# Scheduling weights chosen per stretch of 40 planned microseconds in a two-layer transformer kernel

## The chip, the cores and the metric

The kernel runs on one core of a Trainium2 chip. The core has a matrix engine (TensorE, here PE; its weight loads are listed as PEld), VectorE (DVE), ScalarE (ACT), GpSimd (POOL) and SyncE (SP), which issues most DMAs. Each engine works through its own queue in the order in which the program lists its instructions, and waits on semaphores for the others. The metric is the device time of one execution in microseconds (us), as the median of several runs. A profile comes from one further execution; its span runs from the first to the last recorded instruction.

## What is computed

Two layers over x of shape (1, 2048, 256), in float32. Each has an attention of 16 heads of width 16 with a causal mask, and a gated feed-forward part with int8 weights; each of the four parts sits between two layer norms and is added to x:

```python
x = x + _layernorm(_L0_attn_ref(_layernorm(x, axis=-1), L0_attn_W_d_q, ...), axis=-1)
x = x + _layernorm(_L0_ffn_ref(_layernorm(x, axis=-1), ...), axis=-1)
x = x + _layernorm(_L1_attn_ref(_layernorm(x, axis=-1), ...), axis=-1)
x = x + _layernorm(_L1_ffn_ref(_layernorm(x, axis=-1), ...), axis=-1)
return x
...
scores = jnp.einsum('bhqd,bhkd->bhqk', q, k) / math.sqrt(Hd)
causal = jnp.triu(jnp.full((S, S), -jnp.inf, dtype=scores.dtype), k=1)
scores = scores + causal[None, None]
attn = jax.nn.softmax(scores, axis=-1)
out = jnp.einsum('bhqk,bhkd->bhqd', attn, v)
...
gate = jax.nn.silu(_qmatmul(x, w_gate, s_gate))
up = _qmatmul(x, w_up, s_up)
fuse = gate * up
return _qmatmul(fuse, w_down, s_down)
```

Layer 0's attention draws q and k from low-rank projections with norms and a rotation of their own; layer 1's is the plain one.

## The kernel before

**Tiling.** The 2048 rows are four chunks `c` of 512. Heads are worked on in four groups `g` of four, so that an attention has 16 units `(c, g)`, in the order of `UNITS`: two of chunk 0, all of chunks 1, 2 and 3, then the other two of chunk 0. For each unit, two passes are made:

- *Maxima* (`maxima`, `block`). Blocks of q times k (L766, after two mask products at L762 on the diagonal) go to one PSUM bank each, and VectorE reduces each bank to row maxima (L774). A block uses one half (a "lane") of the array's rows, lane 0 or lane 1; blocks of the two lanes can run at the same time. Unit `(c, g)` has 16c full blocks and ten small ones. POOL splits the maxima into three bf16 parts (L804 to L808), PE turns them (L820) and ACT copies them out (`mrow`, L824).
- *Weighting* (`weighted`). For each of its 4(c+1) key tiles, two score ops subtract the maxima and form the scores (L852 and L857, in two banks), ACT takes the exponential (L863, into `pt`, a ring of six), POOL masks the diagonal ones (L867), and one "weigh" multiplies by the values (L874, eight matmuls). At the end of a unit the result is copied (L882), turned (L887) and divided (L894 to L896).

PE ops have a mode: "row" (maxima and scores), "col" (weighs), "full" (all else). Around these, a chunk's projection (norm, flips at L548, products at L632, `stacked` at L572 and L574) writes q and k to DRAM in SP's stores at L584, and SP loads them back in another layout (`load_stack`, L595) into K and one of three Q buffers. The feed-forward part multiplies at L1027 (gate and up) and L993 (down), with ACT, VectorE and POOL between them (L1034 to L1039). The end of one stage overlaps the start of the next: layer 1's first projection and first maxima are planned inside layer 0's feed-forward part.

**The planner.** All this work is given as ops to a `Plan`, one for each of the four stages (attention 0, feed-forward 0, attention 1, feed-forward 1). An op has an engine, a booked duration in us, a rank (when it is wanted; one unit of attention is 1.0), and buffers it reads, writes or holds. `order` walks through planned time: at each step it works out when each ready op could start (`at`), from its inputs' planned ends, the buffers and PSUM banks that come free, and its engine; for PE with a booked cost for a change of mode (`SWITCH`). It takes the engine of the op that can start first, and among that engine's ops that can start at most `near` us later it picks the one of the least `rank + waiting * (at - first)`. That order of ops is then the order of the instructions on every engine's queue, SP's and POOL's among them. Nothing of it is computed on the chip.

Booked durations that are spoken of below: a score op nq/1110 (0.461 for 512 columns), a weigh nq/590 (0.868), a full maxima block 0.233, its reduction 0.61, the exponential 0.1 + nq/620; a store of q or k 0.6 per part and 3.0 to land, a load of a stack 1.8 and 2.5 to land; `SWITCH` 0.23 into row, 0.1 into col, 0.2 into full.

`run` plans each stage 15 times, with five values of `near` and three of `waiting`, and keeps the pair of the shortest planned stage.

Of the kernel before, what the change touches and what calls it, by code (L numbers as in the profile page):

```python
# [81 lines left out]
class Ring:  # L82
# [3 lines left out]
        self.slots, self.at, self.ordered = [None] * n, 0, ordered  # L86
        self.asked, self.given = [], 0

    def soonest(self, b, others, later):

        if self.ordered and self.asked[self.given + others] is not b:
            return None
        old = self.slots[(self.at + others) % len(self.slots)]
        users = [u.end for u in old.users] if old else [-1.0]
        return None if None in users else max(users)
# [7 lines left out]
class Banks:  # L103
# [15 lines left out]
        at = [self.ready(i) for i in range(len(self.slots))]  # L119
        return [(max(at[i:i + k]), i) for i in range(len(at) - k + 1) if None not in at[i:i + k]]  # L120

    def pairs(self):

        return sum(self.ready(i) is None and self.slots[i].banks == 2 for i in range(len(self.slots))) // 2

    def soonest(self, b, others, later):


        if b.banks == 2 and (self.asked[self.given] is not b or self.pairs() == self.limit):
            return None  # L130
        if later and b.banks == 1:
            used = sum(self.ready(i) is None and self.slots[i].banks == 1 for i in range(len(self.slots)))
            if used + others >= self.singles:
                return None
        free = sorted(t for t, _ in self.choices(b.banks))
        return free[others] if len(free) > others else None

    def give(self, b, now):
# [8 lines left out]
class Places:  # L147
# [9 lines left out]
        users = [b.users if b else () for b in self.slots]  # L157
        return [(max((u.end for u in us), default=-1.0), i) for i, us in enumerate(users) if all(u.end is not None for u in us)]

    def soonest(self, b, others, later):  # L160

        free = sorted(t for t, _ in self.choices())
        others += self.left if later else 0
        return free[others] if len(free) > others else None

# [13 lines left out]
class Plan:  # L179
# [7 lines left out]
    free, mode = {}, None  # L187
    LAG = {"DVE": 0.08, "ACT": 0.1, "PE": 0.2}

    NEAR, WAITING = (0.05, 0.08, 0.11, 0.14, 0.17), (0.05, 0.1, 0.2)  # L190

    def __init__(self):
        self.ops = []
# [16 lines left out]
        self.ops.append(o)  # L210
        return o

    def order(self, near, waiting, emit=False):

        rings = {b.ring for o in self.ops for b in o.bufs if b.ring is not None}
        before = [(r, list(r.slots), r.at, r.given) for r in rings]
        free, mode, left, follow, ready = dict(Plan.free), Plan.mode, {}, {}, []
        for o in self.ops:
            o.end = None
            for b in o.bufs:  # L220
                b.given = b.tile is not None
        for o in self.ops:
            left[o] = sum(d.end is None for d in o.after)
            for d in o.after:
                follow.setdefault(d, []).append(o)
            if left[o] == 0:
                ready.append(o)
        done = 0
        while ready:
            best = []  # L230
            lowest = {2: min((o.rank for o in ready if o.pair and not o.pair.given), default=math.inf),
                      3: min((o.rank for o in ready if o.wide and not o.wide.given), default=math.inf)}
            for o in ready:
                at = max((d.end + self.HOP for d in o.after), default=0.0)
                wanted = {}
                for b in o.bufs:
                    if b.ring is None or b.given:
                        continue
                    others = wanted.get(b.ring, 0)
                    wanted[b.ring] = others + 1  # L240
                    soonest = b.ring.soonest(b, others, o.rank > lowest[3 if b.banks == 3 else 2])
                    if soonest is None:
                        break
                    at = max(at, soonest + self.HOP)
                else:
                    if o.engine == "PE":
                        lanes, more = (o.lanes, 0.0) if o.mode == mode else ((0, 1), self.SWITCH[o.mode] + o.load - self.LOAD)
                        at = max([at + o.load] + [free.get(("PE", x), 0.0) + more for x in lanes])
                    else:
                        at = max(at, free.get(o.engine, 0.0))  # L250
                    best.append((at, o))
            assert best, "nothing can start"
            first = min(best, key=lambda p: p[0])
            at, o = min((p for p in best if p[1].engine == first[1].engine and p[0] <= first[0] + near),
                        key=lambda p: (p[1].rank + waiting * (p[0] - first[0]), p[0]))
            for b in o.bufs:
                if b.ring is not None and not b.given:
                    b.ring.give(b, at)
                b.given = True
                if emit:  # L260
                    b.t
            if emit:
                o.fn()
            if o.engine == "PE":
                mode = o.mode
                for x in (0, 1):
                    free["PE", x] = at + o.us if x in o.lanes else max(at, free.get(("PE", x), 0.0))
            else:
                free[o.engine] = at + o.us
            o.end = at + o.us + o.lag  # L270
            done += 1
            ready.remove(o)
            for n in follow.get(o, ()):
                left[n] -= 1
                if left[n] == 0:
                    ready.append(n)
        assert done == len(self.ops)
        if emit:
            Plan.free, Plan.mode = free, mode
        else:  # L280
            for r, *state in before:
                r.slots, r.at, r.given = state
        return max(o.end for o in self.ops)

    def run(self):

        tried = [(self.order(near, waiting), near, waiting) for near in self.NEAR for waiting in self.WAITING]
        self.span = self.order(*min(tried)[1:], emit=True)


@with_exitstack
def kernel(ctx: ExitStack, tc: tile.TileContext, x_in, cols_in, rows_in, wd_in, wuq_in, rot_in,
# [646 lines left out]
    class FeedForward:  # L939
# [283 lines left out]
```

## Time and profile before

| | |
|---|---|
| median of 3 runs | 1301.8 us (1301.77 to 1302.59) |
| the profiled execution's own time | 1301.22 us |
| its span | 1299.5 us |
| mean granted clock of TensorE | 0.973 |
| first and last weigh (L874) of attention 0 | 85.1 and 540.5 us |
| first and last weigh of attention 1 | 711.2 and 1179.5 us |

The weighs mark the stages: attention 0 runs to about 560 us, feed-forward 0 to about 700, attention 1 to about 1195, feed-forward 1 to the end, with overlaps.

How to read the views: the page lists, for each engine, its busy time and its number of instructions; the slices show 40 equal parts of the span, each digit a busy share in tenths. A row by window gives the window, its length, then the busy time and count of PE, PEld, DVE, ACT and POOL, then the granted clock, the DMA share and GB/s. A row of waits names who waited for whom, the total in us, how often, and the longest. The timeline and the chain give start, length, engine, line and count. Matmuls are pipelined, so that the time from one's start to the next's start is shorter than the recorded length.

### The profile page before, as it was taken

How to read it: one execution, taken by the hardware profiler on the slowest of the kernel's cores; microseconds unless marked ns; L12 is line 12 of the kernel's file. 1: busy time of each engine (PE TensorE's matmuls, PEld its weight loads, DVE VectorE, ACT ScalarE, POOL GpSimd, SP SyncE). 2: the span in 40 equal slices, each digit the busy share in tenths (PEclk: the TensorE clock that was granted, in tenths of full speed). 3: DMA queues.
4: the chain of work that ended last, by engine and by line, in shares of the span. 5: the costliest groups of instructions: out<-in, count | busy, mean ns of one | idle time of the engine just before them, and what ended most of it. 6: DMA issues, size and time to landing. Idle time of an engine off the chain costs nothing.

```text
span 1299.5 us, 22976 instructions
## 1 busy us (share of the span) xinstructions
PE 1213.0 (93%) x8888; PEld 683.8 (53%) x8888; DVE 902.0 (69%) x1714; ACT 792.0 (61%) x1100; POOL 333.6 (26%) x640
## 2 busy tenths in 40 slices
PE   4889999999999999989977999999999999998995
PEld 3655554544444444568755555454445444445884
DVE  4579888888987972264445878978898888334442
ACT  3344665576676678776433656556655777885653
POOL 6021211211102102375423211121101201134564
PEclk8889999999999999999997999999999999998998
DMA  5554260000000000000164051022000000000000
GB/s 153 178 179 128 68 195 17 18 17 17 2 16 18 17 1 18 26 25 1 39 215 120 1 163 33 17 90 74 18 17 18 17 1 18 17 1 1 1 33 33
DMA packets 43486, 65.70 MB, mean 51 GB/s; under 512 B 10739, under 2 KB 15440, under 8 KB 43376
## 3 DMA queue, kind: packets, MB, share of 16 engines
q1 hardware_dynamic: 43040, 63.80, 15.8%
q8 instruction: 70, 1.15, 0.4%
q10 hardware_dynamic: 288, 0.31, 0.1%
q0 software_dynamic: 48, 0.11, 0.1%
q14 instruction: 40, 0.33, 0.1%
HBM read 41.14 MB, written 23.07 MB: 49 GB/s over the span
## 4 chain that ended last, share of the span: by engine, by line
PE 70%; DVE 15%; ACT 5%; issue 3%; DMA 3%; POOL 2%; SPq 2%; POOLq 0%; ACTq 0%; DVEq 0%
PE banks L874 17%; DVE pm L774 12%; PE banks L852 10%; PE banks L766 10%; PE banks L857 8%; PE banks L632 8%; PE banks L1027 7%; PE banks L993 3%; ACT pt L863 3%; PE banks L762 3%; PE banks L548 1%; DMA sc_q<-wide 1%; PE banks L887 1%; ACT wide L523 1%; DMA x<-in_x_dram 1%
## 5 line engine op out<-in xcount | busy, mean ns | idle before, releaser
L774 DVE TENSOR_REDUCE pm<-banks 128x1 f32<-128x512 f32 (+1 forms) x1088 | 672.9, 681 | 154.9 <-PE banks L766 145.9
L863 ACT ACTIVATE pt<-banks 128x1024 f32<-128x1024 f32 (+3 forms) x640 | 544.3, 900 | 267.1 <-PE banks L857 240.3
L857 PE MATMUL banks<-Q,K 64*128 64x512 f32 (+3 forms) x1248 | 322.2, 519 | 0.0
L766 PE MATMUL banks<-K,Q 64*128 64x128 f32 (+2 forms) x1728 | 308.5, 358 | 10.8 <-DMA Q<-sc_q 7.1
L874 PE MATMUL banks<-pt,V 128*32 128x512 f32 (+3 forms) x2560 | 301.7, 544 | 0.5 <-DVE pm L774 0.2
L852 PE MATMUL banks<-mrow,sel 64*128 64x512 bf16 (+3 forms) x1280 | 248.3, 354 | 13.0 <-ACT pt L863 8.4
L766 PEld LDWEIGHTS banks<-K,Q 64*128 64x128 f32 x1728 | 200.2, 189 | 89.3 <-DVE pm L774 44.0
L852 PEld LDWEIGHTS <-sel 64*128 64x128 bf16 x1280 | 77.8, 93 | 258.6 <-issue 246.2
L867 POOL TENSOR_SCALAR_AFFINE_SELECT pt<-pt 128x256 f32<-128x256 f32 x256 | 102.8, 406 | 324.9 <-ACT pt L863 322.8
L857 PEld LDWEIGHTS banks<-Q,K 64*128 64x128 f32 x1248 | 136.2, 195 | 3.6 <-issue 2.8
L1027 PE MATMUL banks<-F,F 128*128 128x512 f32 x512 | 130.7, 400 | 1.8 <-DVE fu L1036 1.8
L1027 PEld LDWEIGHTS banks<-F,F 128*128 128x128 f32 x512 | 96.9, 191 | 22.5 <-DVE fu L1036 2.2
L804 POOL TENSOR_SCALAR mx<-best 128x16 bf16<-128x16 f32 x32 | 9.4, 295 | 362.5 <-DVE best L799 362.4
L1036 DVE SCALAR_TENSOR_TENSOR fu<-banks,cols,sl 128x512 f32<-128x512 f32 x64 | 47.4, 749 | 73.1 <-ACT sl L1034 40.4
L874 PEld LDWEIGHTS banks<-pt,V 128*32 128x32 f32 x2560 | 51.4, 108 | 84.4 <-issue 62.7
L1039 POOL TENSOR_TENSOR fl<-fu,fh 128x512 fp32r<-128x512 f32 x64 | 81.9, 1291 | 47.6 <-ACT fh L1038 47.6
L762 PE MATMUL banks<-mask,half 64*128 64x512 bf16 x256 | 68.8, 397 | 0.3
L1038 ACT CAST fh<-fu 128x512 fp32r<-128x512 f32 x64 | 39.5, 621 | 32.5 <-DVE fu L1036 30.8
L993 PE MATMUL banks<-fl,F 128*128 128x512 f32 x128 | 52.3, 408 | 4.8 <-POOL fl L1039 4.8
L993 PE MATMUL banks<-fh,F 128*128 128x512 f32 x128 | 53.2, 416 | 2.3 <-DVE fu L1036 2.3
L1034 ACT ACTIVATE sl<-banks,cols 128x512 f32<-128x512 f32 x64 | 43.2, 688 | 12.2 <-PE banks L1027 12.0
L824 ACT COPY mrow<-banks 128x512 bf16<-128x512 bf16 x32 | 18.7, 591 | 47.9 <-PE banks L820 47.9
(122 smaller groups left out, 954.5 us busy)
## 6 DMA issues: line engine op xcount, KB each, us to landing
K<-sc_k SPq DMA_DIRECT2D x128, 128.0 KB
Q<-sc_q SPq DMA_DIRECT2D x120, 128.0 KB
sc_q<-wide SPq DMA_DIRECT2D x48, 256.0 KB
sc_k<-wide SPq DMA_DIRECT2D x32, 256.0 KB
x<-in_x_dram SPq DMA_DIRECT2D x4, 512.0 KB
out_dram<-x SPq DMA_DIRECT2D x4, 512.0 KB
f<-in_ffn_dram SPq DMA_DIRECT2D x2, 768.0 KB
F<-sc_q SPq DMA_DIRECT2D x8, 128.0 KB
```

What stands on the lines that cost most here:

```text
L632: nc.tensor.matmul(s.t[:, at:at + n], a, b, start=start, stop=stop)
L762: nc.tensor.matmul(s.t.rearrange("p (d k) -> p d k", k=P), half16[b, x, :], mask_qk[b, x, :, :], start=x == 0, stop=False)
L766: nc.tensor.matmul(s.t[:, to:to + k], qb.t[b, i, t * P:(t + 1) * P], layer.K(kc)[b, 2 * g + i, k0:k0 + k], start=not masked, stop=not mask ...
L774: nc.vector.tensor_reduce(dst, src, AX.X, ALU.max)
L852: nc.tensor.matmul(s.t[:, e, 0:nq], sel[b:b + 64, i, :], mrow.t[b:b + 64, off:CH], start=True, stop=False)
L857: nc.tensor.matmul(s.t[:, e, 0:nq], layer.K(kt // TPC)[b:b + 64, 2 * g + i, k * P:(k + 1) * P], qb.t[b:b + 64, i, off:CH], start=False, st ...
L863: plan.op("ACT", 0.1 + nq / 620, lambda s=s, pt=pt, nq=nq: nc.scalar.activation(pt.t[:, :, 0:nq], s.t[:, :, 0:nq], AF.Exp, scale=scale), r ...
L867: plan.op("POOL", 0.41, lambda pt=pt: nc.gpsimd.affine_select(out=pt.t[:, :, 0:P], in_=pt.t[:, :, 0:P], compare_op=ALU.is_ge, fill=0.0, ba ...
L874: nc.tensor.matmul(av.t[32 * j:32 * j + 32, off:CH], Vs[kt // TPC][:, kt % TPC, DV * h:DV * h + 32], pts[kt, j // 2].t[:, j % 2, 0:nq], st ...
L993: nc.tensor.matmul(dn[dh].t, wdn[:, fc, dh * P:(dh + 1) * P], halves[fc][j].t, start=fc == 0 and j == 0, stop=fc == 7 and j == 1)
L1027: nc.tensor.matmul(s.t[:, i, :], w[:, cc, fc * P:(fc + 1) * P], xT[j].t[:, cc, :], start=n == 0, stop=n == 3)
L1039: plan.op("POOL", 1.3, lambda fu=fu, fh=fh, fl=fl: nc.gpsimd.tensor_tensor(fl.t, fu.t, fh.t.bitcast(F32), ALU.subtract), r=[fu, fh], w=[fl ...
```

## The change

`order` no longer gets one pair of weights for the whole stage but a string of letters, one for each 40 planned us (`STRETCH`); the last letter holds beyond its end. A letter (a digit to base 36) names a row of `WEIGHTS`: `near`, `waiting`, and three shifts of rank that count for PE ops only: for ops of a single lane (the maxima blocks), for col ops (the weighs), and for full ops. The strings are constants in the file, one for each stage. `run` plans each stage once. The rest of the change keeps lists from call to call inside one step of the planner (`known`), the time at which an op's inputs are there (`o.ready`), and its ring buffers (`o.needs`). No op, booked duration, rank or buffer is changed.

```diff
-    NEAR, WAITING = (0.05, 0.08, 0.11, 0.14, 0.17), (0.05, 0.1, 0.2)
+    WEIGHTS = (
+        (0.11, 0.1, 0.0, 0.0, 0.0),
+        (0.05, 0.1, 0.0, 0.0, 0.0),
+        (0.17, 0.1, 0.0, 0.0, 0.0),
+        (0.11, 0.2, 0.0, 0.0, 0.0),
+        (0.05, 0.05, 0.0, 0.0, 0.0),
+        (0.25, 0.2, 0.0, 0.0, 0.0),
+        (0.11, 0.1, 0.3, 0.0, 0.0),
+        (0.11, 0.1, -0.3, 0.0, 0.0),
+        (0.11, 0.1, 0.0, 0.2, 0.0),
+        (0.11, 0.1, 0.0, -0.2, 0.0),
+        (0.11, 0.1, 0.0, 0.0, 0.4),
+        (0.11, 0.1, 0.0, 0.0, -0.4),
+        (0.3, 0.1, 0.0, 0.0, 0.0),
+        (0.02, 0.1, 0.0, 0.0, 0.0),
+        (0.17, 0.05, 0.3, 0.1, 0.0),
+        (0.17, 0.2, -0.2, -0.1, 0.3),
+    )
+    STRETCH, CHOICES, runs = 40.0, (
+        "505518b8132bb1b",
+        "1211",
+        "15f1c3a252212",
+        "555"), 0
...
-    def order(self, near, waiting, emit=False):
+    def order(self, choices, emit=False):
...
-            o.end = None
+            o.end, o.needs = None, [b for b in o.bufs if b.ring is not None and b.tile is None]
...
+        def is_ready(o):
+            o.ready = max((d.end + self.HOP for d in o.after), default=0.0)
+            ready.append(o)
...
-        done = 0
+        done, base = 0, max(free.values(), default=0.0)
         while ready:
-            best = []
+            best, known = [], {}
...
-            first = min(best, key=lambda p: p[0])
-            at, o = min((p for p in best if p[1].engine == first[1].engine and p[0] <= first[0] + near),
-                        key=lambda p: (p[1].rank + waiting * (p[0] - first[0]), p[0]))
+            start, first = min(best, key=lambda p: p[0])
+            near, waiting, single, values, full = self.WEIGHTS[int(choices[min(len(choices) - 1, max(0, int((start - base) / self.STRETCH)))], 36)]
+            if first.engine == "PE":
+                shift = {"row": 0.0, "col": values, "full": full}
+                at, o = min((p for p in best if p[1].engine == "PE" and p[0] <= start + near),
+                            key=lambda p: (p[1].rank + (single if len(p[1].lanes) == 1 else shift[p[1].mode]) + waiting * (p[0] - start), p[0]))
+            else:
+                at, o = min((p for p in best if p[1].engine == first.engine and p[0] <= start + near),
+                            key=lambda p: (p[1].rank + waiting * (p[0] - start), p[0]))
...
-        tried = [(self.order(near, waiting), near, waiting) for near in self.NEAR for waiting in self.WAITING]
-        self.span = self.order(*min(tried)[1:], emit=True)
+        choices = self.CHOICES[Plan.runs]
+        Plan.runs += 1
+        self.span = self.order(choices, emit=True)
```

The replaced helper, for PSUM banks (a bank's `soonest` for one buffer):

```diff
+        if self not in known:
+            at = [self.ready(i) for i in range(len(self.slots))]
+            busy = [s.banks for s, t in zip(self.slots, at) if t is None]
+            known[self] = (sorted(t for t in at if t is not None),
+                           sorted(max(p) for p in zip(at, at[1:]) if None not in p), busy.count(2) // 2, busy.count(1))
+        free, free2, pairs, used = known[self]
+        if b.banks == 2:
+            if self.asked[self.given] is not b or pairs == self.limit:
+                return None
+            free = free2
+        elif later and used + others >= self.singles:
+            return None
         return free[others] if len(free) > others else None
```

More of the change, by code (lines that the diff above doesn't have):

```diff
@@ L87, in __init__, with soonest @@
         self.asked, self.given = [], 0
-    def soonest(self, b, others, later):
+    def soonest(self, b, others, later, known):
         if self.ordered and self.asked[self.given + others] is not b:
@@ L120, in choices, with soonest @@
         return [(max(at[i:i + k]), i) for i in range(len(at) - k + 1) if None not in at[i:i + k]]
[L122 to L129, printed above, removed]
-            return None
[L131 to L135, printed above, removed]
+    def soonest(self, b, others, later, known):
+        if self not in known:
[9 more added lines that the diff above has]
+        elif later and used + others >= self.singles:
+            return None
         return free[others] if len(free) > others else None
@@ L158, in choices, with soonest @@
         return [(max((u.end for u in us), default=-1.0), i) for i, us in enumerate(users) if all(u.end is not None for u in us)]
-    def soonest(self, b, others, later):
-        free = sorted(t for t, _ in self.choices())
+    def soonest(self, b, others, later, known):
+        if self not in known:
+            known[self] = sorted(t for t, _ in self.choices())
+        free = known[self]
         others += self.left if later else 0
@@ L226, in order @@
             if left[o] == 0:
-                ready.append(o)
-        done = 0
+                is_ready(o)
+        done, base = 0, max(free.values(), default=0.0)
         while ready:
-            best = []
+            best, known = [], {}
             lowest = {2: min((o.rank for o in ready if o.pair and not o.pair.given), default=math.inf),
@@ L233, in order @@
             for o in ready:
[L234 to L237, printed above, removed]
-                        continue
[L239 to L244, printed above, removed]
-                else:
[L246 to L251, printed above, removed]
@@ L252, in order @@
-            assert best, "nothing can start"
-            first = min(best, key=lambda p: p[0])
-            at, o = min((p for p in best if p[1].engine == first[1].engine and p[0] <= first[0] + near),
-                        key=lambda p: (p[1].rank + waiting * (p[0] - first[0]), p[0]))
+                at = o.ready
+                if o.needs:
+                    wanted = {}
+                    for b in o.needs:
+                        if b.given:
+                            continue
+                        others = wanted.get(b.ring, 0)
+                        wanted[b.ring] = others + 1
+                        soonest = b.ring.soonest(b, others, o.rank > lowest[3 if b.banks == 3 else 2], known)
+                        if soonest is None:
+                            at = None
+                            break
+                        at = max(at, soonest + self.HOP)
+                    if at is None:
+                        continue
@@ new lines, in order @@
+                if o.engine == "PE":
+                    lanes, more = (o.lanes, 0.0) if o.mode == mode else ((0, 1), self.SWITCH[o.mode] + o.load - self.LOAD)
+                    at = max([at + o.load] + [free.get(("PE", x), 0.0) + more for x in lanes])
+                else:
+                    at = max(at, free.get(o.engine, 0.0))
+                best.append((at, o))
+            assert best, "nothing can start"
+            start, first = min(best, key=lambda p: p[0])
+            near, waiting, single, values, full = self.WEIGHTS[int(choices[min(len(choices) - 1, max(0, int((start - base) / self.STRETCH)))], 36)]
@@ L275, in order @@
                 if left[n] == 0:
-                    ready.append(n)
+                    is_ready(n)
         assert done == len(self.ops)
```

## The prediction

> **What bounds the kernel now.** I read the page's busy rows first, then the busy time by window, the waits of one window, the timeline of TensorE, and last the chain of waits. The page, in 40 slices:
>
> ```profile
> PE 1213.0 (93%) x8888; PEld 683.8 (53%) x8888; DVE 902.0 (69%) x1714; ACT 792.0 (61%) x1100; POOL 333.6 (26%) x640
> PE   4889999999999999989977999999999999998995
> DVE  4579888888987972264445878978898888334442
> PEclk8889999999999999999997999999999999998998
> ```
>
> TensorE is the busy engine; VectorE comes within a few tenths of it in the two attention stages. By window (PE, PEld, DVE, ACT, POOL busy, then the granted clock):
>
> ```profile
> 120.00:520.00 400.00, 392.25 (x3223) 189.78 (x3222) 321.95 (x571) 264.99 (x325) 65.80 (x170) 1.00 0.12 39
> 760.00:1160.00 400.00, 391.41 (x3226) 187.62 (x3224) 314.20 (x551) 268.82 (x331) 64.99 (x164) 1.00 0.12 37
> 680.00:720.00 40.00, 30.04 (x209) 20.55 (x209) 23.45 (x55) 14.51 (x22) 13.36 (x32) 0.79 0.39 111
> 1200.00:1280.00 80.00, 80.00 (x363) 66.33 (x363) 36.57 (x66) 48.89 (x85) 48.38 (x42) 0.97 0.04 14
> ```
>
> The first two are the bulk of the attentions, 800 of 1299.5 us. PE is called busy for 98% of them, but a matmul's recorded length covers the pipeline, so start-to-start times have to be read instead. TensorE in the second window's timeline (start, length):
>
> ```profile
> 840.08 0.39 PE L852 MATMUL banks<-mrow,sel 64*128 64x512 bf16 x2
> 840.54 0.39 PE L852 MATMUL banks<-mrow,sel 64*128 64x512 bf16 x2
> 841.52 1.07 PE L874 MATMUL banks<-pt,V 128*32 128x512 f32 x8
> 842.52 1.09 PE L548 MATMUL banks<-ident,y 128*128 128x128 f32 x8
> 844.01 0.40 PE L766 MATMUL banks<-K,Q 64*128 64x512 f32 x2
> 844.25 0.39 PE L852 MATMUL banks<-mrow,sel 64*128 64x512 bf16 x2
> 844.70 0.38 PE L766 MATMUL banks<-K,Q 64*128 64x512 f32 x1
> 845.01 1.07 PE L874 MATMUL banks<-pt,V 128*32 128x512 f32 x8
> ```
>
> From start to start: a full score op (L852 with L857) 0.46 us, a weigh (L874) 1.00 with the way out of its mode, a pair of maxima blocks on both lanes 0.24, one block alone 0.31. Of VectorE's waits in the second window one line matters:
>
> ```profile
> DVE pm L774 <- PE banks L766: 70.0, 68, 6.8
> ```
>
> VectorE stands idle for 70 us waiting for maxima blocks, and yet the window's chain runs through L774 for 12.4% (50 us; 19.0%, 76 us, in the first window): runs such as 20 reductions from 349.61 to 361.73, where blocks wait for the banks that these reductions free. The two engines take turns in being late. That is a matter of order, which is all that this change touches.
>
> **The change part by part.** (1) The kept lists (`known`, `o.ready`, `o.needs`) give the same answers as the calls they replace. They run while the program is written, and put no instruction on the chip: 0 us, with no cover needed. (2) The instruction set is unchanged, so each engine's sum of lengths is too: PE 1213.0 can change only by overlap. Waits carried by instructions of their own can change in number; PE has 72 of 51 ns at L766, 3.7 us, so I allow plus or minus 1 us and take 0. (3) The order changes. Of the 35 letters, 17 (5, 8, a, b, c, f) name weights that the old grid did not have; the second stage has only letters 1 and 2, both old pairs, so its order may be nearly the old one.
>
> How much can order move? In 760 to 1160, rows by form, priced at unhindered start-to-start times: 416/2 = 208 full scores x 0.46 = 95.7; 832/8 = 104 full weighs x 1.00 = 104.0; 352/2 = 176 pairs x 0.24 = 42.2; 24 each of the narrower scores x (0.35 + 0.245 + 0.185) = 18.7; 12 each of the narrower weighs x (0.785 + 0.57 + 0.357) = 20.5; 272 narrow blocks x 0.056, 94 x 0.06 and 88 masks x 0.113 = 30.8; projections and flips (32 x 0.216, 16 x 0.43, 16 x 0.22, 72 x 0.109, 44 x 0.056) = 27.7; and 140 entries into the weighs' mode x 0.09 (0.55 against 0.46 after a score) = 12.6. Sum 352: 48 us of the 400 are single blocks and waits. The same count for 120 to 520 gives 351, so 49. Together 97 us can be moved by order, 4.8 for each 40 us.
>
> What share? Unhindered PE is a floor that VectorE won't allow everywhere (314 and 322 of 400 busy). The trace has the same work under two orders: units 10 to 13 last 168.5 us in layer 0 (first weigh to first weigh of the next, 362.4 to 530.9) and 166.6 in layer 1 (992.8 to 1159.4), 1.9 apart; single units differ by more (unit 12: 41.9 against 36.8, unit 8: 30.9 against 36.4) and mostly cancel. A choice for each stretch picks among such differences. That the planner's picks are real on the chip is spoken for by its prices: it books 0.461 for a score and the chip took 0.46; 1.01 for a weigh with its switch, 1.00; 0.233 for a pair, 0.24; 0.61 for a reduction, 0.608 (16 in 9.73 us at 829.49). Against it speaks that many picks differ by hundredths. Bounds: all of it, -97, and the other way as much lost as one unit's spread in each four-unit group, 5.5 x 6 = +33. I take half a microsecond for each of the 20 stretches, a tenth of the 4.8: **-10 us**. It is nearest to the four-unit rows, which say that orders from one search differ by about 1%.
>
> The other stretches: 1200 to 1280 holds 363 matmuls of mostly 0.227 us start to start, 82 us in 80: nothing to win, 0. The start (first 80 us) and the last 20 us are chains of loads, norms and stores: 0. The handover to layer 1 is not free of order:
>
> ```profile
> 673.12 2.50 DVE pm L774 x4
> 675.72 1.29 SPq L584
> 677.07 1.12 SPq L595
> 678.24 1.30 SPq L595
> 679.58 4.72 DMA F<-sc_q
> 684.30 0.14 issue
> 684.44 0.44 PE banks L766
> ```
>
> A maxima block heads PE's queue from 676.9 until a Q stack lands; the down products (L993) queued behind it wait 7.5 us with it, and then run at half clock (0.43 start to start instead of 0.23, to 690). The planner books 3.0 us for a store to land where the chain shows 6.87 (651.04), and 2.5 for this load where it shows 4.72, so it can't see this stall and has no reason to move it: 0, with bounds of -11 (stall gone) and +11 (another like it).
>
> On SP the order moves too: a load of Q that is put earlier waits for one of three buffers (SP waited 345.9 us for L766 in all, 13 times) and holds the stores and K loads queued behind it. In the middle of the attentions they have whole units of time; at the handover they haven't.
>
> Sum: -10 + 0 + 0 against the profiled execution's 1301.2 (span 1299.5, 1.7 around it), which stands 0.6 below the median: 1301.8 - 10.3, said as **1291.5 us**.
>
> Counting headroom by busy time instead would give 400 - 391.4 and 400 - 392.3, 16 us in all, and a tenth of that 1.6 us: no change. [...]
>
> **The rivals.** *More of it arrives*: a quarter of the 97 us, 24, and so 1277. For it: letters with shifted ranks for whole modes can join weighs, and each of 320 visits to that mode costs 0.2 us (0.09 in, 0.11 out); the six runs of 14 to 20 reductions in the chain. Against: only 8 letters of 35 shift modes, and of those in use f alone shifts single lanes.
>
> *Nothing arrives*: the picks are differences of hundredths that other delays wash out. 1301.8, give or take 2.6. For it: the two layers' 1.9 us. Against: a new order rarely lands on the same time.
>
> *Slower*: one mechanism, a block at the head of PE's queue whose Q stack has not landed. Place: where a unit's Q load follows its store closely (the handover at 640 to 720, and the first units of each layer). The planner thinks the pair of transfers 6 us shorter than the chain shows; any weights that advance maxima by less than that look free to it and stall PE. Price: one more stall like that at 676, 7.5 us, and 3 us of half clock after it, 10.5, with nothing won elsewhere: 1312. It decides once such stalls exceed the 10 us won. For it: the one there is, and clock 0.79 in that window. Against: all of PE's DMA waits of this kind were 7.5 and 7.1 us in the whole execution.
>
> [...]
>
> *It doesn't do what it says*: the letters were found by the planner's own sum, and a stage whose letters equal its old pair keeps its order. For the second stage that is likely; for the whole kernel it falls under "nothing arrives".
>
> **How the numbers follow.** Forecast (3 to 18 us won, 1283 to 1299) 0.42; more 0.17; nothing 0.10; slower 0.31, because the planner prices transfers wrongly and half of its gains hang on hundredths. The measurement can tell about 0.2%, 2.6 us, from no change. Faster 0.59, same 0.10, slower 0.31. The likeliest case's own range is 1283 to 1299. Both signs hold weight, so the range reaches over both, and leaves out a tenth on each side: 1272 to 1314. The bounds of -97 and +33 lie outside it, since they need every unit to go the same way; both bounds of the handover lie inside.
>
> **What would show it.** Right: the same instruction counts; in windows of the same units less of VectorE's wait for L766 (70.0) and shorter runs of L774 in the chain, fewer L766 x1 rows; the FFN windows as before. Units 10 to 13 of each layer shorter by 2 us or more. Wrong: a new row of PE waiting for Q or F from DMA, or more half-clock stretches (slower); the attentions' spans equal and only the handover moved (then the sum is right by luck); or single units changing by 5 us and cancelling (nothing arrives).

## The result, and the profile after

| | before | changed |
|---|---|---|
| median of 4 runs | 1302.19 us | 1293.82 us |
| all runs | 1301.77 to 1303.27 | 1290.08 to 1296.0 |
| ratio, 95% interval | | 0.9929 (0.9915 to 0.9943) |
| profiled execution, span | 1301.22, 1299.5 | 1296.0, 1294.3 |

The change took 8.4 us off, where 10.3 were forecast. Its runs lie further apart than those before, and the profiled one is the longest of them; the first experiment shows a part of why.

The page of the changed kernel (lines of the code stand 44 further down: L774 is now L818, L766 L810, L874 L918, L1036 L1080, L993 L1037):

```profile
PE 1209.7 (93%) x8888; PEld 683.4 (53%) x8888; DVE 904.7 (70%) x1714; ACT 792.2 (61%) x1100; POOL 335.0 (26%) x640
...
PE   4889999999999999989986999999999999998995
...
PE banks L918 18%; PE banks L810 11%; PE banks L896 10%; DVE pm L818 9%; PE banks L901 9%; PE banks L1071 8%; PE banks L676 8%; PE banks L1037 4%; ACT pt L907 2%; PE banks L806 2%; PE banks L592 1%; PE banks L931 1%; SPq L639 1%; DMA x<-in_x_dram 1%; PE banks L864 1%
```

The counts of each engine are those of before, and the sums differ by at most 3.3 us. What has changed is the chain: the reductions (L774, now L818) carried 12.1% of the span and now carry 9%. That is a matter of attention 0: in the first of the windows below their share of the chain fell from 19.0% to 10.0%, in the second only from 12.4% to 11.9%. The same windows as before (PE, PEld, DVE, ACT, POOL busy, then the clock):

```profile
120.00:520.00 400.00, 394.25 (x3241) 189.86 (x3241) 322.98 (x570) 272.26 (x338) 67.39 (x170) 1.00 0.14 43
760.00:1160.00 400.00, 393.75 (x3275) 190.76 (x3274) 317.47 (x558) 272.09 (x338) 68.27 (x175) 1.00 0.10 29
...
680.00:720.00 40.00, 29.63 (x196) 19.42 (x196) 22.82 (x52) 12.83 (x20) 11.48 (x29) 0.79 0.40 119
...
1200.00:1280.00 80.00, 78.14 (x365) 64.50 (x363) 32.37 (x58) 45.59 (x80) 46.17 (x37) 1.00 0.06 19
```

The second window holds 49 more matmuls than before (3275 against 3226); the first 18. The handover to layer 1 (680 to 720) is as bad as it was. The last row's 78.14 (80.00 before) is only a matter of place: the stage runs 6.6 us earlier here, so that the window reaches further into its end. VectorE's waits in the second window (two lines), then in the first:

```profile
DVE pm L818 <- PE banks L810: 56.1, 64, 6.8
DVE r L938 <- PE banks L931: 10.5, 3, 9.1
...
DVE pm L818 <- PE banks L810: 57.8, 65, 6.8
```

The wait for blocks was 70.0 us before in the second, 53.9 in the first: only the second window's starvation fell, and most of what fell came back in another place. The division at a unit's end (L894, now L938) waited 0.2 us before, and now waits 10.5 for TensorE to turn the unit's result (L931, L887 before). All of VectorE's waits in that window come to 79.1 us, where they were 83.9.

To place the win, the span is cut at five start times of the trace: the first maxima block (with its mask products), the gate and up product behind the first 64 of feed-forward 0 (called the 64th below), the first weigh of attention 1, the same product of feed-forward 1, and the end (us in each part):

| kernel | attention 0 | handover | attention 1 | the two together | last part |
|---|---|---|---|---|---|
| before | 522.4 | 134.8 | 500.6 | 635.4 | 87.6 |
| changed | 523.0 | 136.7 | 491.9 | 628.6 | 89.0 |
| changed, second profile (e1) | 519.8 | 137.3 | 491.9 | 629.2 | 89.0 |

At the two products TensorE has the same work behind it in all three. At the first weigh of attention 1 it has not: from the product of feed-forward 0 up to it, the change puts 97 matmuls of maxima blocks (L766) and 16 of L852, where before there were 86 and 12. The rows of the maxima blocks, changed and before:

```profile
576.68:713.43 136.75, 14.93 (x97) 12.82 (x97) 0.93 0.29 89
```

```profile
576.63:711.20 134.57, 13.92 (x86) 12.20 (x86) 0.92 0.29 89
```

At the prices of the prediction this is some 1.2 us (an estimate: ten narrow blocks at 0.056 to 0.06, a full one, two narrow scores at 0.185). So the handover and attention 1 are to be read together.

Together they give 6.2 to 6.8 us, attention 0 nothing or 2.6, and the last part gives back 1.4. Attention 1 by itself shows 8.7, but a part of that was only moved ahead of its first weigh. The planner's own sum of booked times, which the letters were searched for, has attention 0 shorter by 8.5 us, attention 1 by 6.8, the feed-forward parts by 0.2 and 0.4: 15.9 in all.

### The profile page after: what moved, and what is told of

Same layout as the page of the kernel before. It is cut to its first block, busy times and chain, and to the rows that moved or that the text cites. A ratio compares the mean times of both kernels' runs of the same rounds, so it can differ in the third digit from the quotient of the medians.

```text
span 1294.3 us, 22988 instructions
## 1 busy us (share of the span) xinstructions
PE 1209.7 (93%) x8888; PEld 683.4 (53%) x8888; DVE 904.7 (70%) x1714; ACT 792.2 (61%) x1100; POOL 335.0 (26%) x640
## 3 DMA queue, kind: packets, MB, share of 16 engines
q1 hardware_dynamic: 43040, 63.80, 15.9%
## 4 chain that ended last, share of the span: by engine, by line
PE 74%; DVE 12%; ACT 4%; POOL 3%; issue 3%; DMA 3%; SPq 2%; POOLq 0%; ACTq 0%; DVEq 0%
PE banks L918 18%; PE banks L810 11%; PE banks L896 10%; DVE pm L818 9%; PE banks L901 9%; PE banks L1071 8%; PE banks L676 8%; PE banks L1037 4%; ACT pt L907 2%; PE banks L806 2%; PE banks L592 1%; PE banks L931 1%; SPq L639 1%; DMA x<-in_x_dram 1%; PE banks L864 1%
## 5 line engine op out<-in xcount | busy, mean ns | idle before, releaser
L818 DVE TENSOR_REDUCE pm<-banks 128x1 f32<-128x512 f32 (+1 forms) x1088 | 674.6, 682 | 153.1 <-PE banks L810 149.1
L810 PE MATMUL banks<-K,Q 64*128 64x128 f32 (+2 forms) x1728 | 305.1, 360 | 9.0 <-DMA Q<-sc_q 5.7
L918 PE MATMUL banks<-pt,V 128*32 128x512 f32 (+3 forms) x2560 | 302.8, 546 | 1.1 <-POOL pt L911 0.8
L810 PEld LDWEIGHTS banks<-K,Q 64*128 64x128 f32 x1728 | 199.8, 190 | 99.9 <-DVE pm L818 53.0
L901 PEld LDWEIGHTS banks<-Q,K 64*128 64x128 f32 x1248 | 136.7, 197 | 2.8 <-issue 2.1
L918 PEld LDWEIGHTS banks<-pt,V 128*32 128x32 f32 x2560 | 51.6, 108 | 86.4 <-issue 66.2
L1080 DVE SCALAR_TENSOR_TENSOR fu<-banks,cols,sl 128x512 f32<-128x512 f32 x64 | 47.3, 749 | 70.0 <-ACT sl L1078 28.4
L1037 PE MATMUL banks<-fl,F 128*128 128x512 f32 x128 | 52.3, 409 | 5.8 <-POOL fl L1083 5.8
L1037 PE MATMUL banks<-fh,F 128*128 128x512 f32 x128 | 53.6, 419 | 4.1 <-DVE fu L1080 4.1
L610 POOL TENSOR_TENSOR x<-x,wide 128x1024 f32<-128x1024 f32 x16 | 38.0, 2377 | 36.8 <-ACT wide L567 36.8
```

The lines of the kernel that those rows point to most:

```text
L810: nc.tensor.matmul(s.t[:, to:to + k], qb.t[b, i, t * P:(t + 1) * P], layer.K(kc)[b, 2 * g + i, k0:k0 + k], start=not masked, stop=not mask ...
L818: nc.vector.tensor_reduce(dst, src, AX.X, ALU.max)
L901: nc.tensor.matmul(s.t[:, e, 0:nq], layer.K(kt // TPC)[b:b + 64, 2 * g + i, k * P:(k + 1) * P], qb.t[b:b + 64, i, off:CH], start=False, st ...
L918: nc.tensor.matmul(av.t[32 * j:32 * j + 32, off:CH], Vs[kt // TPC][:, kt % TPC, DV * h:DV * h + 32], pts[kt, j // 2].t[:, j % 2, 0:nq], st ...
L1037: nc.tensor.matmul(dn[dh].t, wdn[:, fc, dh * P:(dh + 1) * P], halves[fc][j].t, start=fc == 0 and j == 0, stop=fc == 7 and j == 1)
```

## The experiments

Each kernel is the changed one with other letters or booked times. Its strings are printed on one line here; rows for the letters g, h and i stand at the end of its `WEIGHTS`. "Old pair" means the pair that the planner of before had chosen for the stage. As letters these are g (0.05, 0.2) for attention 0, 4 for feed-forward 0, 2 for attention 1 and h (0.17, 0.05) for feed-forward 1. With g, 4, 2, h the new planner writes the same list of instructions on every engine as the old one.

### The change and its parts

**e1: the change again.**

> The changed kernel once more, beside its parts, to see whether its runs (1290.1 to 1296.0, against 1301.8 to 1303.3 before) differ by place. If the spread comes from the half-clock stretches at the joints between stages, a profile of a run near 1291 shows the same attention marks but fewer half-clock stretches near 116, 570 or 720 us. If it comes from the attentions, their marks move. Ratio about 0.993 either way.

1294.84 us, ratio 0.9934 (0.9922 to 0.9946). This profile (1293.9) and the first (1296.0) are one program. They are 0.8 us apart at the first weigh of unit 1 (97.3 and 98.1), 3.1 at that of unit 2 (112.1 and 115.2), and 3.1 at that of unit 14. In the first profile, a window ahead of unit 2 (its granted clock is the eighth number, 0.70) and two score ops in it:

```profile
108.00:116.00 8.00, 7.91 (x53) 3.42 (x53) 6.05 (x12) 4.45 (x5) 0.00 (x0) 0.70 0.01 3
```

```profile
109.36 0.61 PE L896 MATMUL banks<-mrow,sel 64*128 64x512 bf16 x2
...
110.20 0.65 PE L896 MATMUL banks<-mrow,sel 64*128 64x512 bf16 x2
```

The same window and the same two ops in the second profile:

```profile
108.00:116.00 8.00, 7.91 (x63) 3.48 (x59) 7.69 (x16) 6.53 (x8) 0.00 (x0) 1.00 0.00 1
```

```profile
107.22 0.39 PE L896 MATMUL banks<-mrow,sel 64*128 64x512 bf16 x2
...
107.68 0.39 PE L896 MATMUL banks<-mrow,sel 64*128 64x512 bf16 x2
```

The score ops start 0.84 us apart in the one and 0.46 in the other. In both, PE had stood still for 0.8 us at 104 to 106 (0.82 and 0.81); in the first alone 6.8 us at half clock followed (granted clock 0.50 from 106 to 112, 1.00 again from 113). That one stretch at the start of attention 0 explains 2.3 us of the distance, which is 2.1 at the end of the two spans. Why the clock fell in the one execution and not in the other, after the same gap, the two profiles don't show.

**e2: attention 0 alone.**

```diff
-        "505518b8132bb1b", "1211", "15f1c3a252212", "555"
+        "505518b8132bb1b", "4", "2", "h"
```

> Only attention 0 planned with the new letters, the other three stages with the old pairs. The planner's own sum for this stage falls by 8.5 us. Theory A (every attention keeps about half of what its plan won): -4 us, ratio 0.997. Theory B (from the two profiles' marks: attention 0 was 5.2 us ahead at its 152nd weigh, but even at the 64th gate and up product, so what it wins is lost at the joint to feed-forward 0): 0 us, ratio 1.000. Theory C (the plan holds on the chip): -8.5, ratio 0.9935.

1297.52 us, ratio 0.9958 (0.9942 to 0.9974): 5.5 us of the planned 8.5. Theory A (0.997) lies inside the interval. Theory B (nothing arrives) falls, and so, by little, does C. In its profile attention 0 takes 519.0 us. The first profile of the change, at 523.0, had misled: it had paid 2.3 us for the half-clock stretch above.

**e3: attention 1 alone.**

```diff
+        "g", "4", "15f1c3a252212", "h"
```

> Only attention 1 planned with the new letters. The planner's own sum falls by 6.8 us. Theory A: -3.5 us, ratio 0.9973. Theory B (attention 1 won 8.8 us between its first weigh and the 64th gate and up product behind it): -7 to -9 us, ratio 0.994. Theory C: -6.8, ratio 0.9948, which lies close to B; the two are told apart by the kernel with attention 0 alone.

1299.24 us, ratio 0.9962 (0.995 to 0.9974): 4.9 of the planned 6.8. Theory A (0.9973) fits; B and C lie outside the interval. Attention 1 takes 492.2 us in the profile, as in the change; the handover ahead of it takes 138.9, 4.1 more than before, with the same 11 and 4 matmuls moved into it. Together they take 631.1, which is 4.3 less than before.

**e4: without shifts.**

```diff
-        "505518b8132bb1b", "1211", "15f1c3a252212", "555"
+        "505510201322212", "1211", "1521c30252212", "555"
```

The letters 8, b, f and a are replaced by letters without a shift of rank: 8 and a by 0, which has the same `near` and `waiting`; b and f by 2, which has another `near` than b (0.17, not 0.11) and another `waiting` than f (0.1, not 0.2).

> The new letters with the rank shifts of whole modes set to zero (letters 8, a, b and f become pairs of near and waiting). The planner's own sum is 5.9 us below that of before (568.5 to 564.9 and 499.6 to 498.0), where the change has 15.9. If the chip follows the plan, half to all of that: -3 to -6 us, ratio 0.995 to 0.998, so that most of the win needs the shifts. Rival: the shifts don't matter on the chip and the win comes from varying near and waiting by stretch: ratio 0.993, as the whole change.

1301.51 us, ratio 0.9997 (0.9977 to 1.0017), and 12 runs from 1296.77 to 1311.55. The planned 5.9 us don't arrive. The rival falls clearly: the change doesn't keep its win without these letters, though for b and f the run doesn't part the shift from the pair. The miss lies in attention 0: it takes 529.8 us in the profile, where the plan has it 3.7 shorter than before, while the handover and attention 1 take 633.5, which is 1.9 shorter, as planned (1.8). That profile (1307.56) is of an execution 6 us above the median. Why this kernel scatters so, and why its attention 0 is long, stays open; it shows a half-clock stretch at 382.8 (granted clock 0.83 over 380 to 390; the weigh that starts at 383.01 takes 1.86 us in the chain, the one at 369.84 0.99) with no gap of PE over 0.2 us just ahead of it (PE is busy for 9.81 of the 10 us up to 380).

**e5: feed-forward 1 by its old pair.**

```diff
-        "505518b8132bb1b", "1211", "15f1c3a252212", "555"
+        "505518b8132bb1b", "1211", "15f1c3a252212", "h"
```

> The change with feed-forward 1 planned by its old pair (near 0.17, waiting 0.05) instead of 555. In the three profiles with 555 the time from the 64th gate and up product of that stage to the end was 88.9 to 89.0 us, in the three with the old pair 87.6, though the planner's own sum calls 555 shorter by 0.4. Theory: this joint costs 1.3 us on the chip, so that this kernel ends 1.3 us sooner than the change: ratio 0.9924 to before where the change had 0.9934, and 87.6 us in that stretch. Rival (a matter of where the half-clock stretches fall): 88 to 89 again in this order.

1290.84 us, ratio 0.9912 (0.9898 to 0.9927). The last part takes 88.0 us. Over all profiles it is 89.0 in the three with 555, and 87.6 to 88.0 in the eleven with the old pair. So 555, which the plan calls 0.4 us shorter, costs 1.0 to 1.4 on the chip. Most of it is one wait, ahead of the last down products, for POOL's last halves; in the change, then here, where it is as before:

```profile
PE banks L1037 <- POOL fl L1083: 1.9, 1, 1.9
```

```profile
PE banks L1039 <- POOL fl L1085: 1.0, 1, 1.0
```

The timed difference to e1, 0.22%, is larger than that, but the intervals overlap.

**e6: the end of attention 0 by its old pair.**

```diff
+        "505518b8132gggg", "1211", "15f1c3a252212", "h"
```

> As the last, and attention 0's last four letters replaced by its old pair. The planner's own sum changes by 0.8 us (it calls this a little worse), but the end of the stage is in another order: 20.9 planned us fewer of maxima left behind the unit that ends at the 152nd weigh is not asserted, the marks tell. Theory: in the change the chip loses at the joint to feed-forward 0 what the stretches won (from the 152nd weigh to the 64th gate and up product 51.5 us against 45.5 before, planned 50.9 against 47.4); with the old letters there it keeps 2 to 3 us more, so 1290 to 1291, ratio 0.990. Rival: the mark only moves work from one side to the other, and the total stays, ratio 0.9924 as the last.

1290.49 us, ratio 0.9904 (0.9887 to 0.9921), no different from e5. From the 152nd weigh (where unit 14 begins) to the 64th product it takes 47.4 us where e5 has 51.4, but the weigh comes 4.6 us later than in e5. The rival holds: that mark only moved work from one side to the other, and the theory of a loss at this joint falls.

### Does the plan's sum decide?

**e7: pairs that the plan calls worse**, h for attention 0 and (0.08, 0.1) for attention 1.

```diff
+        "h", "4", "i", "h"
```

> A test of the planner's sum the other way: both attentions planned with single pairs that it calls worse (0.17 and 0.05 for attention 0, +6.9 us; 0.08 and 0.1 for attention 1, +9.8 us; together +16.6). Theory (half to all of a planned difference arrives on the chip): slower by 8 to 16 us, ratio 1.006 to 1.012. Rival (the gain of the change is luck of one order, unconnected with the plan): anywhere within 5 us of before, ratio 0.996 to 1.004.

1325.38 us, ratio 1.0179 (1.0156 to 1.0202): 23 us slower where the plan said 16.6, and more than the theory's 8 to 16. The rival (within 5 us of before) falls. Attention 0 takes 531.6, attention 1 511.6. TensorE's waits of this kernel:

```profile
PE banks L899 <- ACT pt L910: 14.3, 40, 0.9
PE banks L813 <- DMA Q<-sc_q: 12.1, 3, 6.5
```

In the kernel before they were 8.4 (23 times) and 7.1. The second is the mechanism that the prediction gave to its slower rival: the longest wait, 6.5 us, ends at 799, and the granted clock from 795 to 805 is 0.50. So that mechanism exists, with 5.0 us of the 23 by its waits; the change's letters don't set it off.

**e10: other letters with the same planned sum.**

```diff
+        "5ga7gdg5gggeggg", "4", "15f1caa252612", "h"
```

> Other letters of nearly the same planned sum as the change with the old pair in feed-forward 1 (1281.8 against 1282.6), found by a second search that starts from the old pairs and goes over each stage twice; booked times as before. Theory (what the plan wins arrives, whichever letters win it): 1290 to 1293, ratio 0.991 to 0.993. Rival (the win belongs to that one order): it differs from 0.9912 by more than 0.4%.

1291.71 us, ratio 0.9913 (0.9901 to 0.9926), beside e5's 0.9912. (The plan's sum is 1282.0, where e5 has 1282.5.) Nine of the fifteen letters of attention 0 are the old pair's here; attention 1 differs in two of thirteen. Two orders of attention 0 with nearly the same sum take the same time, so the win doesn't belong to the one order of the change. That the sum alone decides isn't shown: e4 speaks against it.

**e11: half the letters of attention 1.**

```diff
+        "g", "4", "15f1c32222222", "h"
```

> Only attention 1 with new letters, and of its thirteen only the first six (15f1c3), the old pair behind them. The planner's own sum for the stage: 5.6 us won, where all thirteen win 6.9. Theory of the prediction (a win of about half a microsecond in every stretch, wherever it lies): 6 of 13 letters give 6/13 of the win of all thirteen (4 to 5 us timed), 2 us, ratio 0.9985. Theory of the plan: 5.6/6.9 of it, 4 us, ratio 0.997.

1299.46 us, ratio 0.9969 (0.9958 to 0.998): 4.0 us, as the plan's share says (5.6 of 6.8), and not the 2 us (0.9985) of a win that lies evenly; that is just outside the interval.

Side by side, planned difference to before against measured (ratio less one, times 1302.5):

| | planned | measured | | planned | measured |
|---|---|---|---|---|---|
| e7 | +16.6 | +23.3 | e2 | -8.5 | -5.5 |
| e4 | -5.9 | -0.4 | e6 | -14.7 | -12.5 |
| e11 | -5.6 | -4.0 | e5 | -15.5 | -11.5 |
| e3 | -6.8 | -4.9 | e10 | -16.0 | -11.3 |
| | | | e1 | -15.9 | -8.6 |

Each measured figure has an interval of 1.4 to 3 us either way. Apart from e4, half to nine tenths of a planned win arrive, and more than all of a planned loss.

### The wait that the plan can't see

TensorE's waits for transfers in the changed kernel, and the handover in its chain:

```profile
PE banks L810 <- DMA F<-sc_q: 7.3, 1, 7.3
...
PE banks L810 <- DMA Q<-sc_q: 5.7, 2, 3.1
```

```profile
674.68 1.90 DVE pm L818 x3
676.57 0.17 SPq L628
...
676.80 1.47 SPq L628
...
678.32 1.62 SPq L639
679.99 0.85 SPq L639
680.88 4.71 DMA F<-sc_q
685.58 0.14 issue
685.72 0.44 PE banks L810
```

It is the stall of before (7.5 for F, 7.1 for Q), hardly touched: SP issues stores and loads until 680.8, the load takes 4.71 us, and a maxima block waits at the head of PE's queue.

**e8: booked times of the transfers as the profiles show them, letters searched again.**

```diff
-        plan.op("SP", 0.6 * len(parts), keep, r=[both], w=[sc], rank=rank, lag=3.0)
+        plan.op("SP", 0.9 * len(parts), keep, r=[both], w=[sc], rank=rank, lag=6.8)
...
-        plan.op("SP", 1.8, go, r=[sc], w=[buf], after=after, rank=rank, lag=2.5)
+        plan.op("SP", 1.8, go, r=[sc], w=[buf], after=after, rank=rank, lag=4.4)
...
+        "59e00d3ah0100d0", "2440", "b158220122222", "h"
```

> The booked times of the transfers set to what the profiles show (a store 0.9 per part and 6.8 to land, a load 4.4 to land, instead of 0.6, 3.0 and 2.5), and the letters of the first three stages searched again under these prices. Theory of the head of the queue (PE stands 7.3 to 8.6 us at a block of the next layer whose Q stack has not landed, since the plan thinks the transfers short): the planner now puts other PE work there, the wait of L766's line for F falls below 3 us and the handover to layer 1 is 5 to 10 us shorter: 1285, ratio 0.987. Rival: nothing else is ready there, so the wait stays as it is, and the kernel ends near the change, ratio 0.993.

1284.5 us, ratio 0.9861 (0.9846 to 0.9876). The time is the theory's, but not by its way. The one wait of TensorE for a transfer of q is:

```profile
PE banks L812 <- DMA F<-sc_q: 7.0, 1, 7.0
```

The wait for F is there still (the rival's half is right), while the waits for Q, 7.1 before, are gone from the list, and the first weighs come at 77.6 (85.1 before) and 701.3 (711.2). Attention 0 takes 517.7, the handover 129.6, attention 1 491.7; the last two together 621.3, where the change had 628.6.

**e9: the booked times alone, with the old pairs.**

```diff
+        "g", "4", "2", "h"
```

> The corrected booked times of the transfers with the old pairs of weights, one for each stage. The kernel with both (corrected times and new letters) was 18 us below before, the change alone 8.4. Theory P (the extra 10 us come from the times alone: the ramp before the first weigh and the handover are ordered better): about 1292, ratio 0.992, first weigh near 77.6 us. Theory L (the times only let the search see what a letter wins there; with the old pairs they move little): within 3 us of before, ratio 0.998 to 1.002, first weigh near 85.

1301.75 us, ratio 0.9993 (0.998 to 1.0005): Theory L for the time. Not for the marks: the first weigh comes at 80.2, and the handover takes only 120.7, but attention 0 takes 536.6 and eats it all. TensorE's waits for transfers and for `pt`:

```profile
PE banks L898 <- ACT pt L909: 15.1, 37, 1.2
PE banks L812 <- DMA Q<-sc_q: 8.9, 2, 6.2
```

No wait for F is left: what e8's theory expected of the right prices happens here, with the old pairs, and the handover is 14.1 us shorter. But there is a new wait of 6.2 us for a Q stack at 174, inside attention 0, and those for `pt` rose from 8.4 to 15.1. Right prices move the work; the search has to find an order that profits. Against this kernel, under the same prices, e8 was planned 16.9 us shorter, and measures 17.3 (1301.75 - 1284.5): the whole of it. No run has e8's letters under the old prices.

**e12: the same prices, three passes of the search.**

```diff
-        "59e00d3ah0100d0", "2440", "b158220122222", "h"
+        "59e00d3ah000010", "2440", "b15822a122222", "h"
```

> Corrected booked times and letters from three passes of the search instead of one (59e00d3ah000010, 2440, b15822a122222, old pair). The planner's own sum is 1.4 us below that of the kernel with one pass. If the plan holds to this size: 1283, ratio 0.985. Rival: differences this small don't arrive: 1284.5 as before, give or take 1.5.

1281.19 us, ratio 0.9835 (0.9823 to 0.9848): 1.6% below before and 1.0% below the change, the shortest of all, and below both forecasts (1283, and 1284.5 give or take 1.5). Of its 3.3 us against e8 the plan had 1.4. Only one transfer still holds TensorE up, and it is a load of K; the kernel's chain at the handover shows it behind the loads that SP issues one by one:

```profile
PE banks L812 <- DMA K<-sc_k: 6.5, 1, 6.5
```

```profile
665.27 2.50 DVE pm L820 x4
...
669.24 1.12 SPq L641
670.40 0.98 SPq L641
671.42 1.03 SPq L641
...
673.45 3.52 DMA K<-sc_k
676.97 0.12 issue
677.09 0.44 PE banks L812
```

The parts of the span again, with the kernels that tell most:

| kernel | attention 0 | handover | attention 1 | the two together | last part |
|---|---|---|---|---|---|
| before | 522.4 | 134.8 | 500.6 | 635.4 | 87.6 |
| e5 | 520.3 | 135.1 | 490.6 | 625.7 | 88.0 |
| e8 | 517.7 | 129.6 | 491.7 | 621.3 | 87.9 |
| e9 | 536.6 | 120.7 | 497.9 | 618.6 | 87.9 |
| e12 | 517.6 | 129.8 | 491.5 | 621.3 | 87.6 |

Against e5, e8 and e12 win 2.6 to 2.7 us in attention 0 (0.9 of it is four matmuls of L993 fewer ahead of the mark, at 0.227 each) and 4.4 in the handover with attention 1. That this comes of loads, which decide when a unit can begin, fits the waits for Q that are gone, but isn't shown: e7, the slowest, has its first weigh earliest of all, at 75.0.

## Why the prediction was right

**The kept lists, and the count of instructions**: 0 us, as said. The lists of instructions with the old pairs are the same; PE's sum went from 1213.0 to 1209.7, more than the 1 us allowed for waits.

**The sum.** Its terms add up to -10; 0.3 of the 10.3 taken off has no term.

**The attentions, -10 us.** Measured 5.5 and 4.9 one by one, 11.5 together with feed-forward 1 left alone (e5). The sign and its place are right: the win lies in the two attentions, in parts that add up. The reason given is that booked times for scores, weighs, pairs and reductions agree with the rows. It fits that a planned win arrives for the most part (e2, e3, e10, e11), as does a planned loss (e7), but no run changes one of these times, so it remains an argument. And it holds for full ops only: the kernel books no score op below 0.38 us, where the prediction's narrow ones took 0.35, 0.245 and 0.185. The size came out near by luck: a tenth of the 97 us was a choice that no row backed. The figure that told the size was the planner's own sum of booked times, 15.9 us for these letters, of which a half to nine tenths arrives; the prediction didn't use it. What failed is the win's shape: "half a microsecond for each of the 20 stretches". Six letters of attention 1 give 4.0 of its 4.9 us (e11), and without the shifts almost nothing is left (e4), although only 8 of 35 letters have them. The prediction held that small number against a large win; by e4 it is what the win hangs on, as far as that run can tell.

**What would show it**: units 10 to 13 were to be shorter by 2 us or more. They take 165.6 in layer 0 (168.5 before) and 165.0 in layer 1 (166.6), so the second falls short. The wait for L766 fell in one window and rose in the other, single blocks likewise (rows of one block in the timelines: 55, before 69, in the second window, 75 and 73 in the first). The reductions' share of the chain fell in the first window, where the wait rose. So the picture of two engines that take turns in being late is borne out by halves: each sign came in one attention, and no wait was found that accounts for the 8.4 us.

**Feed-forward 1 at 0** was wrong in size: the letters 555 cost 1.0 to 1.4 us, 0.9 of it in the wait for POOL. "Nothing to win" was read as nothing to lose.

**The handover at 0**: the stall stayed at 7.3 us, inside its bounds of 11 either way. The part takes 1.9 and 2.5 us more in the change's two profiles, and 4.1 and 4.2 in e3 and e11, whose order is that of before up to feed-forward 0's own end. Some 1.2 us of it is the work that the new letters of attention 1 put ahead of its first weigh. The granted clock in this part was 0.92 before, 0.93 and 0.90 in the change, 0.91 in e3 and e11; what the rest is, the runs don't settle. That the planner left this stall alone because it couldn't see it is borne out by e9, where right prices remove it, and not by e8, where the wait for F is still 7.0 us.

**Headroom** by busy time foretold no change (a tenth of 16 us), and the 8.4 us refute that. The bound of 16 for the two windows isn't refuted: e12, 21 us below before in all, has 13.9 of them in the two attention parts. By start-to-start times there were 97 in the two windows. e12's PE is still called busy for 94% of its span, where before it was 93% of a span 20 us longer: here this share said little of the room left. Recorded lengths overlap: in the profile before, a down product of 0.39 us starts at 691.15 and the next one at 691.38.

**The rivals.** *Slower* needed more stalls at the head of PE's queue; the transfers' waits are 13.0 us in all in the change and 14.6 before. e7 shows that other weights do set them off. *Nothing arrives* falls with the interval of the ratio, 0.9915 to 0.9943. *More* was held possible at 1277, for reasons of modes; 1281 was reached, by giving the search the right transfer times first.

## What to carry to other kernels

Where an order is planned from booked times, check those times against the profile row by row before searching for better weights: here the larger part of a planned win arrived in seven kernels of eight, and where transfers were booked some 2 to 4 us too short, the search found a third less than under the right prices (e5 won 11.5 us, e8 18.0). As a forecast the planned difference was the better guide here, not a share of the idle time: half to nine tenths of it arrived. The stage that PE already filled (80.00 of the 80 us from 1200 to 1280 before) had nothing to win from another order and still lost 1.0 to 1.4 us. Marks inside a stage shift when work is moved across them, the first weigh of attention 1 among them, so wins are to be counted between points with the same work on both sides.

## What the runs showed of the hardware

The granted clock fell to half after a short gap, and not each time: 0.8 us of idle PE at 105 was followed by 6.8 us of half clock in one execution (0.70 over 108 to 116) and by none in another of the same program (1.00 there), and in e4 a stretch of 3.4 us (0.83 over 380 to 390) came after no gap over 0.2. The stretch of 6.8 us cost 2.3 us, about a third of what the change's nine runs lie apart (1290.1 to 1296.5). What decides when it comes was not found.
